# Macaron block on one core: the strands' normalizations, FFN sums, output scales and masks put on ScalarE and GpSimd beside the attention

## The chip, the cores and the metric

One core of one Trainium2 chip. The time is device microseconds (us) of one execution. Engines as the profile names them: PE is TensorE's matrix multiplication (PEld its weight loads), DVE VectorE, ACT ScalarE, POOL GpSimd, SP SyncE, which here only issues DMAs. PEclk is the TensorE clock that the throttle granted, as a share of full speed. L251 is line 251 of the kernel before.

## What is computed

x is (2, 1024, 512) in fp32. The block is a "macaron": half an FFN, attention, half an FFN, each on the normalized x and added to x.

```python
x = x + 0.5 * ffn(layernorm(x))
x = x + attn(layernorm(x))
x = x + 0.5 * ffn(layernorm(x))

def bitnet_linear(x, weight, scale):          # q, k, v and o projections
    s = maximum(mean(abs(weight), axis=1), 1e-8)
    y = einsum('bsi,oi->bso', x, sign(weight / s[:, None])) * (s * scale)
    return nan_to_num(y, nan=0.0, posinf=1e6, neginf=-1e6)

def attn(x):                                  # 32 query heads, 8 key/value heads, head size 16
    q, k, v = (bitnet_linear(x, w, sc) for w, sc in ...)
    p = softmax(q @ k.T / sqrt(16))           # 1024 keys a query
    return bitnet_linear(p @ v, o_weight, o_scale)

def ffn(x):                                   # base layer plus 8 LoRA experts of rank 16
    w = top-2 of softmax(x @ W_router.T), renormalized
    return x @ W_base.T + b_base + 2 * lora(x, w)
```

## The kernel before

**Tiles.** x stays on chip: 2 batches x 2 groups of 512 tokens, each group 4 tiles of 128 tokens x 512 columns (`xg[b, g]`, `xt[:, t, :]`). Most work on a tile is thus one instruction of 128 partitions x 512 elements. The q, k, v and o projections and the scores use numbers split into a rounded part and a remainder (fp32r), so they take two matmuls where one would do.

**The attention** (L831 on) goes through 32 units: a batch, a half of its queries (512) and one of 8 key/value groups with its 4 query heads. A unit is 4 steps, 128 steps in all. A step issues, for three different units at once:
- m: the scores of 8 tiles (queries on partitions, 512 keys), two matmuls each (`m_tile`, L742), whose row maxima DVE takes, negated (L751). They run 5 steps ahead. After a unit's fourth step the maxima are gathered, transposed and sent through a DMA into `mq`.
- e: the scores of 8 tiles the other way round (128 keys on partitions, 512 queries), two matmuls (L781) and a third that subtracts the maxima (L785), then the exp on ACT (L787), as 8 tiles `es`.
- av: the 32 matmuls of the step before's exps with the values (L820) into one PSUM bank for the unit. After the unit's last, `unit_end` copies the bank to `avs` on ACT (L795) and stores it to DRAM.

PSUM has 8 banks: one for av, seven in a ring for all else.

**What sets the order.** The order of instructions on each engine is written out by the program; no scheduler changes it. A step follows a string of turns: FULL when a strand has matmuls ready, BARE when none has, LEAD_IN at the start. Between the attention's turns m, e and A stand slots in which something else may be issued: F for PE, V and W for DVE, C and D for ACT, and one for POOL and one for DMAs after every turn.

What goes in these slots are **strands**: Python generators, one for each tile's chain of work (FFN, normalization, projections, output). A strand yields the engine that its next instruction needs ("P", "v", "a", "g" for POOL, "d" for a DMA on SP), what that comes after, and since when. A planner (`Flow`) counts ticks, 64 for a step, and offers a strand its slot when a table of delays (`LATER`: for instance 16 from an ACT instruction to the DVE one that uses it, 30 from POOL to DVE, 0 from POOL to POOL) says that the data should be there; on POOL two strand instructions stand at least 10 ticks apart (`APART`). It also keeps a stock of buffers: `t=10` for tiles of 128 x 512, `m=3` for masks, six PSUM banks less four during the attention. `flow.free` is false during the attention and true before and after it. Where the planner is wrong about a time, the engine waits: these ticks only order the instructions.

Strands join the attention by step: from its start, `first(1, 0)` and `first(1, 1)`, the first FFN and the q, k, v tiles of batch 1; later `second(0, 0)`, `second(0, 1)` and `second(1, 0)`, the output projection and the second FFN of three of the four groups. Everything of `first(0, 0)` and `first(0, 1)` is spawned before it, and their last tiles reach into it; `final` and `last` of group (1, 1) end after it. Before a unit is placed (loads of its q and k, L687 and L692) `need` (L839) checks that its q and k tiles are finished, and before its first e turn that its v tiles are (`place_v`, L726 and L727, on POOL). If they are not, `need` offers all five engines to the strands again and again, with no attention turn between, until they have been issued.

**The strands that the change touches:**
- `finite` (L226 to L260), nan_to_num of one tile, run for each q, k and v tile and each output tile. With `fast` 0, the case of most tiles: POOL takes the part below zero, clamped (L249, min then max); DVE makes a mask that is 1 where y x 0 is 0, so where y is finite or large but no NaN or infinity (L251); POOL takes the part above zero (L253, max then min) and adds the two (L255); DVE copies y under the mask (`copy_predicated`, L259).
- `ln_T` (L270 on): from the row statistics, DVE adds eps (L278), POOL takes the power -0.5 (L281, `rstd`), then for each of 4 tiles DVE computes xn = (x - mean) x rstd (L288), PE transposes it (L293), ACT copies it (L297), and ahead of q, k and v DVE makes its remainder (L300).
- `base` in `ffn_tiles` (L410 to L434): POOL makes xb = x + bh, bh being half the bias (L414); four matmuls with the base weight (L419) and one with the LoRA part (L423); DVE takes x = 0.5 x pb + xb from the bank (L425); then a store on SP or the row statistics for the next normalization on DVE.
- `qkv_part` (L490 on): matmuls (L504 for q and k tiles, L521 for v), the scale on ACT (L509) or on DVE for v (L526), `finite`, and for q and k the rounded part on ACT (L534), the remainder on POOL (L537) and two stores to DRAM on SP (L543), from where the units load them.
- `o_proj` (L619 to L649): matmuls (L634), DVE scales by the output scale `osc` (L639), `finite`, POOL adds to x (L645), DVE takes row statistics. Its inputs are normalized before it in `normalize` (L561 on), with POOL products at L586 and L590.

Of the kernel before, what the change touches and what calls it, by code (L numbers as in the profile page):

```python
# [32 lines left out]
def macaron_kernel(ctx: ExitStack, tc: tile.TileContext, x_in, wbT, b_base, wrT, aT, bT,  # L33
# [16 lines left out]
    def t512(name, dt=F32):  # L50
        return tmp.tile([P, 512], dt, tag="t512", name=name)
# [174 lines left out]
    def finite(y, o, n, fast, back):  # L226
# [20 lines left out]
        else:  # L247
            yield "g", src, t
            nc.gpsimd.tensor_scalar(lo_, y, 0.0, -BIG, ALU.min, ALU.max)  # L249
            yield "v", src, t  # L250
            nc.vector.tensor_scalar(m_, y, 0.0, 0.0, ALU.mult, ALU.is_equal)  # L251
            yield "g", ""
# [17 lines left out]
    def ln_T(xt, n, mv, given, tiles, xs, rank):  # L270
# [9 lines left out]
        rstd = sm.tile([P, TG], F32, tag="rstd", name=f"rstd{n}{tiles[0]}", bufs=4)  # L280
        nc.gpsimd.tensor_tensor(rstd[:, own], ve[:, own], mhalf[:, own], ALU.pow)  # L281
        at = flow.t

        def part(t):
            yield "r", dict(t=1)
            yield "v", "g", at
            xn = t512(f"xn{n}_{t}")
            nc.vector.tensor_scalar(xn, xt[:, t, :], mv[:, t, 0:1], rstd[:, t:t + 1], ALU.subtract,  # L288
                                    ALU.mult)
            yield "P", "v", None, 1  # L290
            pt = bank(f"pt{n}_{t}").rearrange("p (c q) -> p c q", c=KC)
            for c in range(KC):
                nc.tensor.transpose(pt[:, c, :], xn[:, c * P:(c + 1) * P], ident)  # L293
            flow.give(t=1)
            yield "a", "P"
            tok = slice(t * P, (t + 1) * P)
            nc.scalar.copy(xT[:, :, tok], pt)  # L297
            if xL is not None:
                yield "v", "a"
                nc.vector.tensor_tensor(xL[:, :, tok], pt, xT[:, :, tok].bitcast(F32), ALU.subtract)  # L300
            flow.give(fb=1)
# [18 lines left out]
    def ffn_tiles(xt, name, rank, tiles, xT, hT, mv, given, mv2, summed, store, loads):  # L320
# [89 lines left out]
        def base(t):  # L410
            yield "r", dict(t=1)
            yield "g", ""
            xb = t512(f"xb{n}_{t}")
            nc.gpsimd.tensor_tensor(xb, xt[:, t, :], bh, ALU.add)  # L414
            for c in range(KC):
# [7 lines left out]
            nc.tensor.matmul(pb, hT[0][:, t * P:(t + 1) * P], lb, start=False, stop=True)  # L423
            yield "v", "P"
            nc.vector.scalar_tensor_tensor(xt[:, t, :], pb, 0.5, xb, ALU.mult, ALU.add)  # L425
            flow.give(t=1, fb=1)
            if store is not None:
                yield ("a" if flow.free else "d"), "v"
                (nc.scalar if flow.free else nc.sync).dma_start(store[t * P:(t + 1) * P, :],
                                                                xt[:, t, :])  # L430
            if mv2 is not None:
                yield "v", "v"
                stats(xt, t, mv2, n)
                summed.add(t)  # L434
# [184 lines left out]
    def o_proj(b, g, hs, rank, mv, given, fast=False):  # L619
# [5 lines left out]
        def part(t):  # L625
            yield "r", dict(t=3)
            wo = signs["o"]
            for c in range(KC):
# [7 lines left out]
                flow.lock = ss[t] if c < 2 else None  # L636
            yield "v", "P"
            y = t512(f"yo{n}_{t}")
            nc.vector.tensor_tensor(y, po, osc, ALU.mult)  # L639
            flow.give(fb=1)  # L640
            done.append(t)
            r = t512(f"ro{n}_{t}")
            yield from finite(y[:, :], r[:, :], f"o{n}_{t}", fast, ("v", flow.t))
            yield "v" if fast else "g", "v"
# [186 lines left out]
    def attention(chains, n0):  # L831
# [6 lines left out]

        def need(*keys):  # L839
            for _ in range(4000):  # L840
                flow.settle()
                if set(keys) <= ended:
                    return
# [6 lines left out]
        for n in range(n0, TU * len(units) + LEAD + 1):  # L850
# [12 lines left out]
            for pos, (kind, p, i) in enumerate(order):  # L863
# [7 lines left out]
                elif kind == "A":  # L871
                    if a:
                        a_part(a[0], a[1] * 2 + p // 2, p % 2)
                elif kind == "S":
# [148 lines left out]
```

## Time and profile before

| | us |
|---|---|
| median of 3 runs | 1261.95 (1256.4 to 1266.83) |
| the profiled execution, its own time | 1256.92 |
| its span on the core | 1255.2 |
| 0 to 156 us: load, binarized weights, first FFN and q, k, v of batch 0 | 156; PE 114.33, DVE 111.84, ACT 35.45, POOL 71.54 busy |
| 156 to 1184 us: attention with strands beside it | 1028 |
| 1184 to 1255.2 us: last group's output projection and FFN | 71.2; PE 54.08, DVE 38.67, ACT 6.04, POOL 8.00 busy |
| largest group on DVE: the row maxima, L751 | 1024 x 0.682 = 657.0 busy |
| largest group on ACT: the exps, L787 | 1024 x 0.599 = 546.9 busy |
| mean granted TensorE clock | 0.915 |

The page's first part gives each engine's busy time and its share of the span. A busy engine need not be the one that sets the time: an instruction counts as busy also where nobody waits for it. PE's busy time includes matmuls at a lowered clock, so the same work is longer where PEclk is low. In groups such as `L253 POOL TENSOR_SCALAR z<-y 128x512 ... x17`, the first name is the tile written and the second the tile read, then come the shape, the count, the busy time, the mean of one in ns, and the idle time before them with what ended it. The chain of waits follows the work that ended last back from its end: at each step to whatever released it, or to the instruction before it on its engine. The profile's fences below come in these forms.

### The profile page before, as it was taken

The numbers are of one execution on the slowest core, as the hardware profiler recorded it, in microseconds if no ns is written. First come the engines' busy times: TensorE is split into PE (matmuls) and PEld (weight loads), VectorE is DVE, ScalarE is ACT, GpSimd is POOL, SyncE is SP. The second block draws the span as 40 slices with busy tenths as digits, with TensorE's granted clock in tenths as the row PEclk, the third lists the DMA queues.
The fourth block names the chain that finished last, engine by engine and source line by source line (L and its number), as shares of the span: only waits on it lengthen the run. The fifth ranks groups of instructions, "written<-read, shape, count | busy, mean of one in ns | idle before, by whom it ended". The sixth has DMA issues, their size and how long they took to land.

```text
span 1255.2 us, 25499 instructions
## 1 busy us (share of the span) xinstructions
PE 1148.8 (92%) x10501; PEld 606.1 (48%) x10501; DVE 902.8 (72%) x1733; ACT 641.6 (51%) x1249; POOL 295.0 (24%) x302
## 2 busy tenths in 40 slices
PE   3988699999999999999999999999999999998868
PEld 3546355454454544444554445444455444545434
DVE  5578876767786777776677976777769677895273
ACT  2222255655554665565565666455557655566401
POOL 3135832000000340031555220241000300422110
PEclk8989588899986999987999899899989899999788
DMA  7010332121212222223132241122222422211110
GB/s 254 1 59 34 81 122 85 52 52 52 52 52 52 69 80 57 70 76 89 49 90 75 72 122 53 33 52 69 61 60 67 123 68 65 68 55 38 45 39 34
DMA packets 38708, 85.57 MB, mean 68 GB/s; under 512 B 7728, under 2 KB 10800, under 8 KB 34624
## 3 DMA queue, kind: packets, MB, share of 16 engines
q1 hardware_dynamic: 37184, 81.26, 22.4%
q8 instruction: 82, 1.34, 0.4%
q10 hardware_dynamic: 1152, 2.10, 0.4%
q0 software_dynamic: 256, 0.59, 0.3%
q14 instruction: 34, 0.28, 0.1%
HBM read 59.57 MB, written 23.84 MB: 66 GB/s over the span
## 4 chain that ended last, share of the span: by engine, by line
PE 70%; DVE 19%; issue 3%; DMA 2%; POOL 2%; ACT 1%; SPq 1%; POOLq 0%; ACTq 0%; DVEq 0%
PE av L820 20%; PE m L742 16%; DVE mn L751 11%; PE e L781 10%; PE pbf L419 5%; PE pbs L419 5%; PE e L785 4%; PE po L634 2%; PE phs L342 1%; DMA qd<-y 1%; PE pq L504 1%; PE pbf L423 1%; PE pv L521 1%; PE pbs L423 1%; DMA x<-in_x 1%
## 5 line engine op out<-in xcount | busy, mean ns | idle before, releaser
L751 DVE TENSOR_REDUCE mn<-m 128x1 f32<-128x512 f32 x1024 | 657.0, 682 | 230.0 <-PE m L742 221.4
L787 ACT ACTIVATE es<-e 128x512 f32<-128x512 f32 x1024 | 546.9, 599 | 425.6 <-PE e L785 401.4
L742 PE MATMUL m<-k,q 32*128 32x512 f32 x2048 | 492.1, 464 | 21.1 <-DVE mn L751 15.1
L781 PE MATMUL e<-q,k 32*128 32x512 f32 x2048 | 407.9, 474 | 8.3 <-DVE mn L751 6.9
L742 PEld LDWEIGHTS m<-k,q 32*128 32x128 f32 x2048 | 240.8, 196 | 153.0 <-issue 67.4
L820 PE MATMUL av<-es,vaug 128*32 128x256 f32 x4096 | 290.3, 416 | 16.4 <-issue 10.3
L781 PEld LDWEIGHTS e<-q,k 32*128 32x128 f32 x2048 | 185.1, 194 | 114.7 <-DVE mn L751 69.6
L785 PE MATMUL e<-mq,ones_r 2*128 2x512 f32 x1024 | 233.0, 431 | 3.7 <-DMA mq<-mT 3.7
L820 PEld LDWEIGHTS av<-es,vaug 128*32 128x32 f32 x4096 | 121.5, 116 | 154.5 <-issue 103.8
L785 PEld LDWEIGHTS e<-mq,ones_r 2*128 2x128 f32 x1024 | 125.6, 196 | 25.1 <-issue 13.7
L419 PE MATMUL pbf<-wb,xTf 128*128 128x512 f32 x128 | 68.9, 653 | 1.3 <-DVE mn L751 1.3
L419 PE MATMUL pbs<-wb,xTs 128*128 128x512 f32 x128 | 64.8, 618 | 1.2 <-DVE mn L751 1.2
L586 POOL TENSOR_TENSOR an<-an,rb 128x512 f32<-128x512 f32 x15 | 19.2, 1281 | 142.7 <-DMA rd<-rs 72.1
L249 POOL TENSOR_SCALAR loa<-y 128x512 f32<-128x512 f32 x17 | 12.7, 750 | 157.1 <-ACT y L509 147.5
L726 POOL MEMSET vaug<- 128x128 f32 x32 | 6.6, 206 | 137.7 <-PE av L820 137.6
L419 PEld LDWEIGHTS pbf<-wb,xTf 128*128 128x128 f32 x128 | 23.2, 203 | 30.1 <-issue 26.1
L419 PEld LDWEIGHTS pbs<-wb,xTs 128*128 128x128 f32 x128 | 21.5, 189 | 27.1 <-issue 22.9
L253 POOL TENSOR_SCALAR z<-y 128x512 f32<-128x512 f32 x17 | 34.1, 2008 | 1.8 <-DMA qd<-y 0.6
L249 POOL TENSOR_SCALAR loo<-yo 128x512 f32<-128x512 f32 x12 | 7.4, 613 | 113.7 <-DVE yo L639 110.0
L537 POOL TENSOR_TENSOR z<-z,y 128x512 fp32r<-128x512 f32 x17 | 21.9, 1293 | 51.0 <-ACT y L534 51.0
L590 POOL TENSOR_TENSOR anxL<-an,anxT 128x512 fp32r<-128x512 f32 x15 | 19.2, 1280 | 53.5 <-ACT anxT L588 53.4
L634 PE MATMUL po<-sign_o,anxT 128*128 128x512 f32 x64 | 29.4, 459 | 1.2 <-DVE mn L751 1.2
(193 smaller groups left out, 1008.3 us busy)
## 6 DMA issues: line engine op xcount, KB each, us to landing
k<-kd SPq DMA_DIRECT2D x31, 1024.0 KB
q<-qd SPq DMA_DIRECT2D x32, 256.0 KB
ad<-avs SPq DMA_DIRECT2D x32, 256.0 KB
x<-in_x SPq DMA_DIRECT2D x16, 256.0 KB
qd<-y SPq DMA_DIRECT2D x16, 256.0 KB
qd<-z SPq DMA_DIRECT2D x16, 256.0 KB
an<-ad SPq DMA_DIRECT2D x15, 256.0 KB
rb<-rd SPq DMA_DIRECT2D x15, 256.0 KB
```

The source lines that it names most:

```text
L249: nc.gpsimd.tensor_scalar(lo_, y, 0.0, -BIG, ALU.min, ALU.max)
L253: nc.gpsimd.tensor_scalar(o, y, 0.0, BIG, ALU.max, ALU.min)
L419: nc.tensor.matmul(pb, xT[:, c, t * P:(t + 1) * P], wb[:, c, :], start=(c == 0), stop=False)
L423: nc.tensor.matmul(pb, hT[0][:, t * P:(t + 1) * P], lb, start=False, stop=True)
L537: (nc.vector if fast else nc.gpsimd).tensor_tensor(lo, o, y, ALU.subtract)
L634: nc.tensor.matmul(po, hs[j][:, c, t * P:(t + 1) * P], wo[:, c, :], start=(c + j == 0), stop=(c + j == KC))
L742: nc.tensor.matmul(s["m", i], s["q"][rows, qt * P:(qt + 1) * P], s["k"][rows, 1 - p, kh * 512:(kh + 1) * 512], start=(p == 0), stop=(p == 1))
L751: nc.vector.tensor_reduce(s["mn"][:, h, qt, kh:kh + 1], s.pop(("m", i)), AX.X, ALU.max, negate=True)
L781: nc.tensor.matmul(t, s["k"][rows, 1 - p, kt * P:(kt + 1) * P], s["q"][rows, :], start=(p == 0), stop=False)
L785: nc.tensor.matmul(t, ones_r[two, :], s["mq"][two, :], start=False, stop=True)
L787: nc.scalar.activation(e, s.pop(("e", i)), AF.Exp, scale=HD ** -0.5)
L820: nc.tensor.matmul(s["av"][32 * h:32 * h + 32, cols], s["v"][:, kt, :], s["es"][kt * REP + h][:, cols], start=(kt + half == 0), stop=(kt + ...
```

## The change

Beside the attention (`flow.free` false), and for the mask wherever `finite` runs with `fast` 0, work of the strands changes engine:
- the mask is computed by POOL, right after the part below zero, in place of DVE;
- a normalization computes, once for each `ln_T`, neg = -mean x rstd in two small POOL instructions, and each xn is one ACT instruction, Identity with scale rstd and bias neg, in place of DVE;
- an FFN tile adds bh to x in place on POOL; ACT then copies half the bank to a tile `hb`, and POOL adds that to x, in place of DVE's sum from the bank;
- an output tile is copied from its bank by ACT and multiplied by `osc` in place on POOL, in place of DVE's product.

`need` becomes a case of a new `until(cond)`, which also stands ahead of a unit's first av turn: until the copy of the unit before's av bank has been issued, it offers the engines to the strands.

```diff
--- before.py
+++ after.py
@@ -247,8 +247,8 @@
         else:
             yield "g", src, t
             nc.gpsimd.tensor_scalar(lo_, y, 0.0, -BIG, ALU.min, ALU.max)
-            yield "v", src, t
-            nc.vector.tensor_scalar(m_, y, 0.0, 0.0, ALU.mult, ALU.is_equal)
+            yield "g", ""
+            nc.gpsimd.tensor_scalar(m_, y, 0.0, 0.0, ALU.mult, ALU.is_equal)
             yield "g", ""
             nc.gpsimd.tensor_scalar(o, y, 0.0, BIG, ALU.max, ALU.min)
             yield "g", "g"
@@ -279,15 +279,26 @@
         yield "g", "v"
         rstd = sm.tile([P, TG], F32, tag="rstd", name=f"rstd{n}{tiles[0]}", bufs=4)
         nc.gpsimd.tensor_tensor(rstd[:, own], ve[:, own], mhalf[:, own], ALU.pow)
+        calm = not flow.free
+        if calm:
+            yield "g", ""
+            neg = sm.tile([P, TG], F32, tag="neg", name=f"neg{n}{tiles[0]}", bufs=4)
+            nc.gpsimd.tensor_tensor(neg[:, own], mv[:, own, 0], rstd[:, own], ALU.mult)
+            yield "g", ""
+            nc.gpsimd.tensor_scalar(neg[:, own], neg[:, own], -1.0, None, ALU.mult)
         at = flow.t
 
         def part(t):
             yield "r", dict(t=1)
-            yield "v", "g", at
+            yield "a" if calm else "v", "g", at
             xn = t512(f"xn{n}_{t}")
-            nc.vector.tensor_scalar(xn, xt[:, t, :], mv[:, t, 0:1], rstd[:, t:t + 1], ALU.subtract,
-                                    ALU.mult)
-            yield "P", "v", None, 1
+            if calm:
+                nc.scalar.activation(xn, xt[:, t, :], AF.Identity, bias=neg[:, t:t + 1],
+                                     scale=rstd[:, t:t + 1])
+            else:
+                nc.vector.tensor_scalar(xn, xt[:, t, :], mv[:, t, 0:1], rstd[:, t:t + 1],
+                                        ALU.subtract, ALU.mult)
+            yield "P", "a" if calm else "v", None, 1
             pt = bank(f"pt{n}_{t}").rearrange("p (c q) -> p c q", c=KC)
             for c in range(KC):
                 nc.tensor.transpose(pt[:, c, :], xn[:, c * P:(c + 1) * P], ident)
@@ -410,8 +421,7 @@
         def base(t):
             yield "r", dict(t=1)
             yield "g", ""
-            xb = t512(f"xb{n}_{t}")
-            nc.gpsimd.tensor_tensor(xb, xt[:, t, :], bh, ALU.add)
+            nc.gpsimd.tensor_tensor(xt[:, t, :], xt[:, t, :], bh, ALU.add)
             for c in range(KC):
                 yield ("P", "P") if c else ("P", "", flow.t, 1)
                 if c == 0:
@@ -421,15 +431,24 @@
                 flow.lock = bs[t] if c < KC - 1 else None
             yield "P", "a", ready
             nc.tensor.matmul(pb, hT[0][:, t * P:(t + 1) * P], lb, start=False, stop=True)
-            yield "v", "P"
-            nc.vector.scalar_tensor_tensor(xt[:, t, :], pb, 0.5, xb, ALU.mult, ALU.add)
-            flow.give(t=1, fb=1)
+            if flow.free:
+                yield "v", "P"
+                nc.vector.scalar_tensor_tensor(xt[:, t, :], pb, 0.5, xt[:, t, :], ALU.mult, ALU.add)
+                flow.give(t=1, fb=1)
+            else:
+                yield "a", "P"
+                hb = t512(f"hb{n}_{t}")
+                nc.scalar.activation(hb, pb, AF.Copy, scale=0.5)
+                flow.give(fb=1)
+                yield "g", "a"
+                nc.gpsimd.tensor_tensor(xt[:, t, :], xt[:, t, :], hb, ALU.add)
+                flow.give(t=1)
             if store is not None:
-                yield ("a" if flow.free else "d"), "v"
+                yield ("a" if flow.free else "d"), "v" if flow.free else "g"
                 (nc.scalar if flow.free else nc.sync).dma_start(store[t * P:(t + 1) * P, :],
                                                                 xt[:, t, :])
             if mv2 is not None:
-                yield "v", "v"
+                yield "v", "v" if flow.free else "g"
                 stats(xt, t, mv2, n)
                 summed.add(t)
 
@@ -634,13 +653,19 @@
                     nc.tensor.matmul(po, hs[j][:, c, t * P:(t + 1) * P], wo[:, c, :],
                                      start=(c + j == 0), stop=(c + j == KC))
                 flow.lock = ss[t] if c < 2 else None
-            yield "v", "P"
+            yield "v" if fast else "a", "P"
             y = t512(f"yo{n}_{t}")
-            nc.vector.tensor_tensor(y, po, osc, ALU.mult)
+            if fast:
+                nc.vector.tensor_tensor(y, po, osc, ALU.mult)
+            else:
+                nc.scalar.copy(y, po)
             flow.give(fb=1)
             done.append(t)
+            if not fast:
+                yield "g", "a"
+                nc.gpsimd.tensor_tensor(y, y, osc, ALU.mult)
             r = t512(f"ro{n}_{t}")
-            yield from finite(y[:, :], r[:, :], f"o{n}_{t}", fast, ("v", flow.t))
+            yield from finite(y[:, :], r[:, :], f"o{n}_{t}", fast, ("v" if fast else "g", flow.t))
             yield "v" if fast else "g", "v"
             (nc.vector if fast else nc.gpsimd).tensor_tensor(xt[:, t, :], xt[:, t, :], r, ALU.add)
             flow.give(t=2)
@@ -837,9 +862,12 @@
         live = []
 
         def need(*keys):
+            until(lambda: set(keys) <= ended)
+
+        def until(cond):
             for _ in range(4000):
                 flow.settle()
-                if set(keys) <= ended:
+                if cond():
                     return
                 flow.t += 1
                 for kind in "Pvagd":
@@ -870,6 +898,8 @@
                         e_tile(e[0], e[1] * 2 * REP + i, p)
                 elif kind == "A":
                     if a:
+                        if a[0] and a[1] == p == 0:
+                            until(lambda: "av" not in st[a[0] - 1])
                         a_part(a[0], a[1] * 2 + p // 2, p % 2)
                 elif kind == "S":
                     if 0 < hold <= len(units):
```

The built program of the kernel after has 89 instructions fewer on DVE (21 q, k and v masks, 12 o masks, 16 FFN sums, 28 normalizations, 12 output scales), 56 more on ACT and 77 more on POOL (33 masks, 12 products, 16 sums, 16 small ones for neg); PE has as many as before, SP too.

## The prediction

> **What bounds the kernel now.** I read first the page's busy times and the clock row, then a table of stretches, then single groups, and last the one place where batch 0 hands over to batch 1.
>
> ```profile
> PE 1148.8 (92%) x10501; PEld 606.1 (48%) x10501; DVE 902.8 (72%) x1733; ACT 641.6 (51%) x1249; POOL 295.0 (24%) x302
> ...
> PEclk8989588899986999987999899899989899999788
> ```
>
> PE is the full engine; DVE has a quarter of its time free, ScalarE half, GpSimd (POOL) three quarters. That average hides stages, so I cut the span: the attention runs from 156 to 1184 us, 128 steps of 8 exps each (1024 exps), 1028/128 = 8.03 us a step. Three single steps, by stretch (columns as named; PEclk is the granted clock):
>
> ```profile
> core 0: us, PE busy (x) PEld busy (x) DVE busy (x) ACT busy (x) POOL busy (x), PEclk, DMA share, GB/s
> 156.00:1184.00 1028.00, 980.43 (x9838) 505.66 (x9839) 752.29 (x1390) 600.10 (x1154) 215.44 (x222) 0.93 0.24 67
> 278.40:285.70 7.30, 7.30 (x80) 3.46 (x84) 5.00 (x9) 4.24 (x8) 0.00 (x0) 1.00 0.01 2
> 363.80:369.40 5.60, 5.60 (x75) 2.74 (x77) 5.60 (x11) 4.28 (x8) 0.00 (x0) 1.00 0.12 47
> 923.60:933.00 9.40, 9.40 (x75) 3.90 (x77) 4.87 (x8) 4.36 (x8) 0.00 (x0) 0.51 0.01 3
> ```
>
> The first step has strand matmuls between the attention's: PE 7.30 of 7.30, DVE 5.00. The second has none: PE and DVE both cover it. The third is the same work at half clock: 9.4 us. So in a filled step DVE work is free until about 7.3 us; in a bare step it shows; and PE that lets go loses its clock. Of 128 steps 99 are filled and 29 bare, in both programs by the built order. Followed through 156 to 1184 us, the chain of waits gives the operations that the change takes from DVE only 1.4 (o masks), 1.2 (output scales), 1.1 (normalizations) and 0.8 us (q/k/v masks). But POOL has 13.5 us on that chain, most of it in one place, where the q/k tiles of batch 1 come due before its first unit:
>
> ```profile
> 623.54 1.28 POOL L537 TENSOR_TENSOR z<-z,y 128x512 fp32r<-128x512 f32 x1 [0.26 <-ACT y L534]
> 624.91 0.97 POOL L249 TENSOR_SCALAR loa<-y 128x512 f32<-128x512 f32 x1
> 625.96 1.97 POOL L253 TENSOR_SCALAR z<-y 128x512 f32<-128x512 f32 x1
> 628.01 1.29 POOL L255 TENSOR_TENSOR z<-z,loa 128x512 f32<-128x512 f32 x1
> 629.38 1.13 POOL L249 TENSOR_SCALAR loa<-y 128x512 f32<-128x512 f32 x1
> 630.58 1.92 POOL L253 TENSOR_SCALAR z<-y 128x512 f32<-128x512 f32 x1
> 632.58 1.28 POOL L255 TENSOR_TENSOR z<-z,loa 128x512 f32<-128x512 f32 x1
> ```
>
> and, in the chain of waits (start, length, what), its release:
>
> ```profile
> 633.89 0.73 DVE z L259
> 634.63 0.58 DVE mn L751
> 635.20 0.04 issue
> 635.25 0.49 PE m L742
> ```
>
> POOL is solid, DVE's copy (L259) stands waiting for it, the row maxima behind that copy wait, and PE, whose banks they hold, stands 1.43 us.
>
> **What the change takes away.** DVE loses 89 instructions: 21 q/k/v masks x 0.60, 12 o masks x 0.68, 16 FFN sums x 0.685, 28 normalizations x 0.61 and 12 output scales x 0.676, that is 12.6 + 8.1 + 11.0 + 17.1 + 8.1 = 57 us (means of their rows).
>
> ```profile
> L251 DVE TENSOR_SCALAR ma<-y 128x512 uint8<-128x512 f32 x17 | 10.3, 605 | 0.7 <-ACT y L509 0.7
> ...
> L639 DVE TENSOR_TENSOR yo<-po,osc 128x512 f32<-128x512 f32 x16 | 10.8, 676 | 0.7 <-PE po L634 0.7
> ```
>
> On the path lie 4.5 us of these by the chain. Bounds: 0, and about 29 us, if every o mask, output scale and second normalization (8.1 + 8.1 + 12 x 0.74) fell in a bare step. I take 6: the sums sit in filled steps like the one above, where even a sum and its statistics (1.54 us) leave DVE at 6.5 of 7.3.
>
> **What it adds to ScalarE.** 28 normalizations, 16 half-copies, 12 output copies. The copy from a bank is 0.60 (L795); the scaled evacuation L509 0.69; with a second per-row operand an estimated 0.78. Together 28 x 0.78 + 28 x 0.60 = 39 us on an engine busy 600 of 1028. Each may hold an exp, and so a bank, for its length; between 0 and 8 us of the path, I take 2. Behind them queue the exps and the copy of the finished sums (L795); the next unit's first sum waits for that copy in either program.
>
> **What it adds to POOL.** 33 masks, 12 scale products and 16 sums (1.28 each, as L586), 16 tiny negations (at most 1.04 each, the 128x4 power of L281). The mask on POOL has no row. Two-operation scalar rows of its shape are 0.61 (L249: min, max) and 1.92 to 2.0 (L253: max, min). The Trainium skill ("GPSIMD Engine Reference", section 4.1) has it that one-input work runs there at about line rate and only two-input work costs twice DVE's. L249 fits it; L253, also one-input, is at three times L249. By the rule a mask is 0.6; by L253 1.95. I take 1.95: it makes a flag and is no min-max pair, so the general row is nearer; both ends stay for the range. In-place sums with bh only free a buffer.
>
> **The handover, step by step.** Let T be the end of the last K tile's matmuls (606.1 before). In the built order that tile stands one step later, the V tile and three q tiles follow with hardly any attention work between, and four dependent copies (K, V, q0, q1) stand back to back in DVE's queue, ahead of all further maxima. As in the trace, POOL starts at T+3.0 and the V tile reaches it at T+12 (before: 617.89). Until then POOL does K: 0.69 + 1.97 + 2.0 + 1.37, and two attention products, 2.6, ready at T+11.6. From T+12: V 6.0 with its mask, q0 6.4 with its mask, an attention product 1.3, the low half of q1 1.2, K's remainder 1.35, and q1's mask, clamp and sum 5.3: together 21.6, so T+33.6. DVE copy 0.73 and one maximum 0.58: PE goes on at T+35. PE itself ends V at T+9.2, three q tiles (24 x 0.23 = 5.5) at T+14.9, and with 7 banks in turn gets about half a step (3 us) on: it stands from T+18 to T+35, 17 us, where it stood 1.9 before. **+15** (at 0.6 a mask: +11). K's and q's loads queue on SP behind these tiles' stores; the first unit of batch 1 uses them four steps later, so they stay covered: k16 was issued at 628 and first needed at 654, and moves no more than the stall.
>
> The rule that weighs against such a hole is in "TensorE: Matmul & The Clock Gate", Part 1: an idle window of 3.4 us throttles the clock to half until a busy window has passed. By it the restart costs up to 3.4 us at half speed, 1.7 us lost; by the row 923.60:933.00, a whole step at 0.51, 3.8. I take **+2**.
>
> **The o tiles.** POOL had 5.1 us each (0.61 + 1.92 + 1.32 + 1.28); with scale, mask and gaps 8.8. In the second and third groups they come one a filled step (7.45 us), so each puts POOL 1.35 us further back. The hand planner leaves 94 of 64 ticks a step, 10.9 us, from the ScalarE copy to the masked copy; the first needs 8.1, the fourth 12.2. 1.3 us late, three groups, some of it covered: **+2** (0 to 8).
>
> **The start** (109 to 153 us) is POOL-bound until 127.6 and DVE-bound after. Three masks ahead of the first waited copy put it at 128.7; DVE then has less to do and the first row statistics are out about 1.8 us sooner, but the next masked copy, behind six masks, ends at 156.5 and holds DVE. I take 0 (-6 with cheap masks, +1). After 1184 us nothing that runs there changes but the in-place sum: 0.
>
> **Sum.** 1256.9 (profiled; span 1255.2) - 6 + 2 + 15 + 2 + 2 + 0 = 1271.9. The median of the runs, 1261.95, lies 5 above that execution: **1277**.
>
> **Rivals.**
> *Cheap masks* (0.6 us). Then -6 - 5 (start) + 2 + 11 + 2 + 0 - 4 (o stages, where DVE is lighter and POOL in time) = 0: about 1262. For it: L249. Against: L253.
> *DVE was the real bound in the o and bare stages.* For it: 11.9% of the attention's chain are maxima, and steps with output tiles take 8.7 to 11 us. Then -29, the handover only +8 since DVE comes to it with no backlog: about 1241, faster. It decides from about 20 us of DVE work on the path. Against: bare steps with 0.87 and with 1.27 us of such work both take 5.61.
> *POOL becomes the bound more widely*: the masked copies of four q/k/v tiles more and of all 12 o tiles wait for a mask each, 16 x 1.95 = 31: about 1308. Against: 222 POOL instructions take 215 of 1028 us.
> That the work is not moved is excluded: the built program has the counts above.
>
> **How the numbers follow.** Mine 0.52 (own range 1266 to 1292), cheap masks 0.20, DVE bound 0.15, POOL bound 0.13. A change of under 1% can hardly be told from none in this kernel. Over 1% slower is above 1274.6: 0.40 of mine and the last, 0.53. Faster by over 1% (under 1249.3): the third and a rest of the second, 0.18. Between: 0.29. Range with one in ten out on each side: 1247 to 1305.
>
> **What would show it.** POOL's mask rows at about 1.95 us (0.6: the first rival). A hole on PE of over 10 us near 620 to 650 us, ended by DVE's L259 after POOL's L255 of the second q tile, with a half clock behind it. DVE's wait for POOL at L259 well above 5.8 us. Filled steps still at 7.3 us though DVE has less. I am wrong if the hole is absent, or if the o stages shorten by over 10 us.

## The result, and the profile after

The kernel after takes 1274.33 us (median of 12 runs, 1261.56 to 1295.88), the kernel before 1261.02 (12 runs). The ratio is 1.0084, interval 1.0055 to 1.0112 (comparisons here leave disturbed runs out): 10.6 us slower, where +15 was forecast. The profiled execution took 1261.77 us (span 1260.0) and is at the fast end of its runs, with a granted clock of 0.920 where the nine runs compared average 0.912; so its stages are compared with before's, and totals come from the runs.

The page of the kernel after, its busy times and its clock row:

```profile
PE 1142.7 (91%) x10501; PEld 603.4 (48%) x10501; DVE 859.7 (68%) x1644; ACT 673.3 (53%) x1305; POOL 399.1 (32%) x379
...
PEclk8989589999998989997979989999979999999689
```

DVE has 43 us less, ACT 32 more, POOL 104 more: the work moved as counted. The 57 us that the prediction took from DVE are counts times means; busy time counts instructions that overlap once, so it falls by less. (For the same reason 1024 maxima of 0.682 us make the 657.0 us busy of the table before, and not 698.) The table of stretches (columns as in the prediction): the attention's window, a filled step, a bare step, and then steps 55 and 56 at the handover to batch 1, which before took 23.8 us:

```profile
156.00:1184.00 1028.00, 973.22 (x9802) 504.52 (x9806) 716.27 (x1313) 630.17 (x1206) 312.62 (x297) 0.93 0.24 68
331.30:338.60 7.30, 7.30 (x80) 3.46 (x79) 5.80 (x11) 4.23 (x8) 0.00 (x0) 1.00 0.00 0
700.40:706.00 5.60, 5.60 (x76) 2.86 (x72) 5.52 (x10) 4.92 (x9) 5.44 (x6) 1.00 0.50 135
605.60:647.10 41.50, 27.71 (x213) 17.80 (x209) 16.01 (x25) 13.64 (x26) 37.46 (x27) 0.75 0.19 48
```

Filled and bare steps last as long as before, 7.3 and 5.6 us. In the last row POOL is busy 37.46 of 41.50 us and PE 27.71. POOL's timeline there (start, length, what), by the built order from the K tile on:

```profile
607.33 0.62 POOL L249 TENSOR_SCALAR loa<-y 128x512 f32<-128x512 f32 x1 [6.81 <-ACT y L528]
608.01 1.93 POOL L251 TENSOR_SCALAR ma<-y 128x512 uint8<-128x512 f32 x1
610.02 1.93 POOL L253 TENSOR_SCALAR z<-y 128x512 f32<-128x512 f32 x1
...
615.88 0.95 POOL L249 TENSOR_SCALAR loa<-yv 128x512 f32<-128x512 f32 x1
...
632.28 1.93 POOL L251 TENSOR_SCALAR ma<-y 128x512 uint8<-128x512 f32 x1
634.27 1.93 POOL L253 TENSOR_SCALAR z<-y 128x512 f32<-128x512 f32 x1
636.28 1.26 POOL L255 TENSOR_TENSOR z<-z,loa 128x512 f32<-128x512 f32 x1
```

and in the chain of waits the release at its end:

```profile
637.57 0.73 DVE z L259
638.30 0.58 DVE mn L776
638.89 0.04 issue
638.93 0.79 PE m L767
```

The K tile's matmuls end at 604.43 (T). POOL began at T+2.9, the V tile reached it at T+11.5, the copy that releases PE came at T+33.1 and PE went on at T+34.5; the prediction had T+3.0, T+12, T+33.6 and T+35. PE stood 8.26 us from 623.5 and 5.50 from 633.4. Before, the eight steps around this place (steps 50 to 57, each counted from its first exp) took 79.6 us; after, 96.1: +16.5. The waits in 603 to 650 us name both holders:

```profile
DVE z L259 <- POOL z L255: 15.7, 3, 7.0
...
PE e L806 <- ACT es L812: 8.3, 1, 8.3
ACT y L553 <- DVE z L259: 7.6, 1, 7.6
...
PE m L767 <- DVE mn L776: 5.5, 1, 5.5
```

Only the second gap is the predicted one, DVE's maxima behind a copy. In the first, exps stand behind ACT's rounding of a q tile (L553), which waits for DVE's copy of that tile, which waits for POOL: the same chain through another queue.

A second hole was not predicted. ACT stood 5.28 us before the fourth normalization of the second FFN, at 744.5 us:

```profile
744.50 0.81 ACT L296 ACTIVATE xns<-x,negs,rstds 128x512 f32<-128x512 f32 x1 [5.28 <-POOL an L605]
```

Its inputs had been there for long. None of them comes from the POOL product (L605) that released it, so the wait must be for the tile that it writes: one of the ring of 128x512 tiles, which that product still read. The product itself waited 4 us for a DMA. Before, DVE met this wait for 1.0 us and PE did not stop; on ACT the exps stand behind it. PE stopped 3.35 us, until 745.86, and the half clock lasted 17.1 us, from 744.9 on. Steps 70 to 72, around it, take 31.3 us where before they took 20.2.

### The profile page after: what moved, and what is told of

Read it like the earlier page. It is cut to its first block, busy times and chain, and to the rows that moved or that the text cites. A ratio compares the mean times of both kernels' runs of the same rounds, so it can differ in the third digit from the quotient of the medians.

```text
span 1260.0 us, 25519 instructions
## 1 busy us (share of the span) xinstructions
PE 1142.7 (91%) x10501; PEld 603.4 (48%) x10501; DVE 859.7 (68%) x1644; ACT 673.3 (53%) x1305; POOL 399.1 (32%) x379
## 4 chain that ended last, share of the span: by engine, by line
PE 66%; DVE 12%; POOL 10%; DMA 5%; issue 4%; ACT 1%; SPq 1%; POOLq 0%; DVEq 0%; ACTq 0%
PE av L845 17%; PE m L767 15%; PE e L806 10%; DVE mn L776 6%; PE pbf L429 5%; PE pbs L429 4%; PE e L810 4%; DMA rd<-rs 3%; PE po L653 2%; PE pq L523 2%; POOL ma L251 1%; PE phs L353 1%; PE pbf L433 1%; PE pbs L433 1%; POOL z L253 1%
## 5 line engine op out<-in xcount | busy, mean ns | idle before, releaser
L845 PE MATMUL av<-es,vaug 128*32 128x256 f32 x4096 | 282.7, 408 | 8.5 <-DVE idfs L386 3.6
L810 PE MATMUL e<-mq,ones_r 2*128 2x512 f32 x1024 | 230.3, 430 | 2.0 <-DMA mq<-mT 2.0
L845 PEld LDWEIGHTS av<-es,vaug 128*32 128x32 f32 x4096 | 118.7, 114 | 143.2 <-issue 88.4
L444 POOL TENSOR_TENSOR x<-x,hbf 128x512 f32<-128x512 f32 x8 | 10.2, 1280 | 174.4 <-ACT hbf L441 174.4
L605 POOL TENSOR_TENSOR an<-an,rb 128x512 f32<-128x512 f32 x15 | 19.2, 1285 | 123.8 <-DMA rb<-rd 121.8
L444 POOL TENSOR_TENSOR x<-x,hbs 128x512 f32<-128x512 f32 x8 | 10.3, 1283 | 106.1 <-ACT hbs L441 106.1
L249 POOL TENSOR_SCALAR loa<-y 128x512 f32<-128x512 f32 x17 | 13.7, 804 | 87.5 <-ACT y L528 86.9
L424 POOL TENSOR_TENSOR x<-x,bh 128x512 f32<-128x512 f32 x32 | 40.8, 1305 | 0.0
L259 DVE COPY_PREDICATED z<-ma,y 128x512 f32<-128x512 uint8 x20 | 21.1, 1055 | 24.7 <-POOL z L255 24.6
L553 ACT CAST y<-z 128x512 fp32r<-128x512 f32 x20 | 12.5, 623 | 44.5 <-DVE z L259 41.3
```

Source lines behind the costliest of these rows:

```text
L424: nc.gpsimd.tensor_tensor(xt[:, t, :], xt[:, t, :], bh, ALU.add)
L810: nc.tensor.matmul(t, ones_r[two, :], s["mq"][two, :], start=False, stop=True)
L845: nc.tensor.matmul(s["av"][32 * h:32 * h + 32, cols], s["v"][:, kt, :], s["es"][kt * REP + h][:, cols], start=(kt + half == 0), stop=(kt + ...
```

## The experiments

Each kernel is the one named with the edit shown; ratios are to the kernel before on the same chip. Theory A: the masks on POOL make the loss at the handover (A1 by POOL's serial time, A2 by the order that is built there). B: normalizations on ACT hold exps. C: POOL's load everywhere. D: DVE is the bound, so whatever lightens it gains. For the parts that gain, later: E, the sums loosen the order at the handover; F, the scales relieve DVE in the output tiles.

**Masks back on DVE** (kernel after):

```diff
-            yield "g", ""
-            nc.gpsimd.tensor_scalar(m_, y, 0.0, 0.0, ALU.mult, ALU.is_equal)
+            yield "v", src, t
+            nc.vector.tensor_scalar(m_, y, 0.0, 0.0, ALU.mult, ALU.is_equal)
```

> The kernel after, but every mask on DVE again; normalizations, FFN sums and output scales stay moved. In the built order the tiles at the handover to batch 1 stand as before the change: the V tile and three q tiles in separate steps, maxima between the four masked copies. Theory A (the masks make the loss, most of it in the hole at the handover, where PE stands 8.3 and 5.5 us in the kernel after and some 17 us are at half clock behind it): no gap on PE over 3 us between 600 and 650 us, and the time falls below the kernel before, by the 44 us that DVE still loses, of which 3 to 8 us lie on the path: ratio 0.994 to 0.999. Theory B (ScalarE's new work holds exps and banks, above all the wait at 742 us): the time stays above before, ratio 1.003 to 1.008.

Measured: ratio 0.9804 (0.9754 to 0.9853), median 1237.22. PE's longest gap at 600 to 650 us is 1.74 us. A's direction holds: the masks make the whole loss, and more. But the gain, 25 us, is three times the 8 us at A's far end: in this company the masks cost 0.028, some 35 us, and the other moves gain 25. Steps 50 to 57 in the kernel after and then in this one:

```profile
560.20:656.30 96.10, 78.67 (x678) 44.15 (x677) 51.77 (x85) 46.48 (x87) 49.54 (x39) 0.80 0.28 83
```

```profile
558.60:630.00 71.40, 66.95 (x662) 37.57 (x660) 51.13 (x87) 43.23 (x82) 39.03 (x33) 0.93 0.30 88
```

They differ by 24.8 us. The two profiles differ by 23.8 in all (spans 1260.0 and 1236.2), so as far as the profiles show, the masks' cost lies at the handover.

**Masks back at the handover only** (kernel after; the six tiles of batch 1, group 1):

```diff
-            yield "g", ""
-            nc.gpsimd.tensor_scalar(m_, y, 0.0, 0.0, ALU.mult, ALU.is_equal)
+            if n[:4] != "a1_1":
+                yield "g", ""
+                nc.gpsimd.tensor_scalar(m_, y, 0.0, 0.0, ALU.mult, ALU.is_equal)
+            else:
+                yield "v", src, t
+                nc.vector.tensor_scalar(m_, y, 0.0, 0.0, ALU.mult, ALU.is_equal)
```

> The kernel after with the masks of the six tiles of batch 1, group 1 alone back on DVE; 27 masks stay on POOL. The built order at the handover stays the one of the kernel after: K one step later, V and three q tiles in one step, four masked copies nearly back to back ahead of the maxima. Theory A1 (POOL's serial time for these tiles is the hole): POOL has 4 x 1.95 = 7.8 us less before the copy that releases PE, so the two gaps of 13.8 us together shrink to about 6, and the time falls by 8 to 12 us against the kernel after, to a ratio of 0.999 to 1.002 to before. Theory A2 (the order, with copies back to back, makes the hole, whatever a mask costs): the gaps stay over 11 us and the ratio over 1.005. Theory C (POOL's load of masks everywhere costs): six of 33 masks are worth 2 us, ratio 1.006.

Measured: 1.0039 (1.0001 to 1.0077), median 1268.82; gaps 5.42 and 2.88 us, 8.3 in place of 13.8. Gaps and ratio both lie between the ranges of A1 and A2. So 5.5 us of the hole go with the masks' serial time (A1, 7.8 expected), and the rest stays with the built order (A2): K a step later, V and three q tiles in one step, copies back to back.

**Cheap masks** (kernel after, same order):

```diff
-            nc.gpsimd.tensor_scalar(m_, y, 0.0, 0.0, ALU.mult, ALU.is_equal)
+            nc.gpsimd.tensor_scalar(m_, y, 1.0, 1.0, ALU.min, ALU.max)
```

> The kernel after in exactly its order; only the mask's operation on POOL is another, min with 1 and then max with 1, so that the mask is always 1 and a NaN or an infinity is no longer replaced: that part of the computation is left out. It asks whether the general two-operation form is what makes a mask dear (the min-max pair took 0.61 us at L249). If such a mask takes 0.6 to 0.8 us: theory A expects 4 x 1.2 = 5 us less hole at the handover (8 to 9 us of gaps), 4 to 6 us less before 150 us and 0 to 4 in the output tiles, together ratio 0.996 to 1.001, as the rival with cheap masks was worked out (1262 where before is 1262). If POOL were not on the path, nothing changes: ratio 1.008. If it still takes 1.9 us, the price is that of the flag tile, not of the pair, and nothing changes.

Measured: 0.9995 (0.9971 to 1.0018), the first rival's time, no change. By form, the mask's row in the kernel after and then in this one:

```profile
L251 POOL TENSOR_SCALAR ma<-y 128x512 uint8<-128x512 f32 x17 | 32.9, 1935 | 1.0
```

```profile
L251 POOL TENSOR_SCALAR ma<-y 128x512 uint8<-128x512 f32 x17 | 10.4, 613 | 1.0
```

The pair of operations sets the price, 1.94 against 0.61 us, and not the flag tile, which both kernels write. The first exp comes 7 us sooner than in the kernel after (147.7 for 154.6 us), and the gaps at the handover are 5.8 and 4.2 us.

**Second normalizations on DVE** (kernel after):

```diff
-        calm = not flow.free
+        calm = not flow.free and n[0] != "s"
```

> The kernel after with the 12 normalizations of the second FFN back on DVE, all else as after; its order up to 700 us is that of the kernel after, so the hole at the handover stays. Theory B (in the profile after, ACT stood 5.3 us at 739 us before the fourth of these, which waits for a tile that a POOL product still reads, which itself waits for a DMA; exps stood behind it, PE stood 3.35 us and then ran 17 us at half clock): that gap goes, and the steps 70 to 72 fall from 31 to about 20 us; ratio 1.000 to 1.004. Theory A: the gap goes but the clock makes up for it elsewhere and DVE takes 12 x 0.74 = 9 us again, ratio 1.006 to 1.010.

Measured: 0.9976 (0.9951 to 1.0001), median 1257.47, 13.6 us below the kernel after by the ratios and at or below B's range. Steps 70 to 72 fall from 31.3 to 21.8 us. No gap over 1 us is left from 650 to 900 us and the half clock behind it is gone; the hole at the handover stays (8.27 and 5.49). D falls here: DVE got 9 us of work back and the kernel is faster.

**Masks and second normalizations back** (kernel after, the first edit and the last):

```diff
-            yield "g", ""
-            nc.gpsimd.tensor_scalar(m_, y, 0.0, 0.0, ALU.mult, ALU.is_equal)
+            yield "v", src, t
+            nc.vector.tensor_scalar(m_, y, 0.0, 0.0, ALU.mult, ALU.is_equal)
...
-        calm = not flow.free
+        calm = not flow.free and n[0] != "s"
```

> The kernel after with all masks and the 12 normalizations of the second FFN back on DVE; still moved are 16 normalizations of batch 1, the FFN sums and the output scales. Theory B (an ACT normalization that waits for a tile holds exps, PE stops and loses its clock): the gap and half clock that the kernel with the masks back still had at 707 to 736 us go, time lost to the clock 85 to 92 us where it was 94; ratio 0.972 to 0.980. Theory D (what made the kernel with the masks back fast is the lighter DVE): 9 us of DVE work come back, ratio 0.983 to 0.990.

Measured: 0.9792 (0.9748 to 0.9835). Against masks back alone (0.9804) the second normalizations make no difference that can be told, though the half clock at 726 us went (10.2 to at most 3.4 us) and steps 70 to 72 fell from 27.2 to 19.9 us; other steps gave it back. The price of 13.6 us was one of the two changes together. B's range holds, but its cause is not shown here.

**Sums and scales only** (kernel after, all masks and normalizations back):

```diff
-            yield "g", ""
-            nc.gpsimd.tensor_scalar(m_, y, 0.0, 0.0, ALU.mult, ALU.is_equal)
+            yield "v", src, t
+            nc.vector.tensor_scalar(m_, y, 0.0, 0.0, ALU.mult, ALU.is_equal)
...
-        calm = not flow.free
+        calm = False
```

> The kernel after with all masks and all normalizations back on DVE; only the 16 FFN sums and 12 output scales stay on ACT and POOL. In its built order the handover is looser than in both kernels: the q tiles come one a step, with maxima between all masked copies. Theory A and B (moved masks and moved normalizations each cost, sums and scales gain): no gap over 2 us at 570 to 640 us, ratio 0.970 to 0.982. Theory D: 17 us of DVE work come back against the kernel with the masks back, ratio 0.984 to 0.992.

Measured: 0.9836 (0.9794 to 0.9878), at the edge between the theories: with 17 us of DVE work more than with the masks back it is 4 us slower by the ratios, whose intervals overlap. No gap over 1 us is left from 210 to 720 us, so the handover has no hole. But at 726.0 us PE stops for 4.0 us, 13.7 us of half clock follow, and steps 70 to 72 take 31.3 us, as in the kernel after, with no normalization on ACT at all:

```profile
728.83 0.62 ACT L607 CAST anxT<-an 128x512 fp32r<-128x512 f32 x1 [4.94 <-POOL an L605]
```

This is the rounded copy of the product itself, which every kernel makes on ACT; here it stands ahead of exps, and the product waits 4.0 us for the DMA. So theory B is too narrow: the second hole does not need a moved normalization, only an ACT instruction ahead of the exps that waits for the late product.

**Masks only** (kernel before):

```diff
-            yield "v", src, t
-            nc.vector.tensor_scalar(m_, y, 0.0, 0.0, ALU.mult, ALU.is_equal)
+            yield "g", ""
+            nc.gpsimd.tensor_scalar(m_, y, 0.0, 0.0, ALU.mult, ALU.is_equal)
```

> The kernel before with the masks on POOL and nothing else. In its built order the V tile and three q tiles stand in separate steps and maxima stand between the four masked copies, as before. Theory A1 (POOL's serial time, 1.95 us a mask): the copy of the fourth tile still comes 7.8 us later, PE's gaps between 600 and 660 us sum to 5 to 9 us, where before had 1.9; time without the clock's loss 4 to 8 us up, ratio 1.003 to 1.008. Theory A2 (the hole comes from the compressed order that masks and normalizations moved together give): gaps under 4 us there, ratio 0.996 to 1.002. Theory D: DVE 21 us lighter, ratio under 0.995.

Measured: 1.0014 (0.9993 to 1.0035). The waits of PE at 600 to 660 us:

```profile
PE m L742 <- DVE mn L751: 5.5, 3, 2.9
```

5.5 us, the longest 2.9: the gaps lie in A1's range, the ratio in A2's. Alone, in the loose order, moved masks cost next to nothing in all. By stage, that is a cost and gains: steps 50 to 57 take 89.0 us (79.6 before), the first two groups of output tiles, steps 58 to 65 and 73 to 82, 59.9 and 83.2 (62.8 and 87.3 before). On top of sums and scales they cost 0.015 (the next kernel against the last), on top of the normalizations too, 0.028.

**No normalizations moved** (kernel after):

```diff
-        calm = not flow.free
+        calm = False
```

> The kernel after with all 28 normalizations back on DVE; masks, sums and scales stay moved. Its built order at the handover is the loose one. Theory B: as with the second normalizations back, the clock's loss is 90 to 97 us in place of 112; with the looser handover the gaps there are 4 to 9 us in place of 13.8; ratio 0.984 to 0.993. Theory A1 alone (POOL's masks make the loss and the order does not matter): gaps still over 10 us and ratio 0.997 to 1.003.

Measured: 0.9987 (0.9964 to 1.0009): the ratio lies in A1's range, above B's, and the gaps lie in B's. The order is loose, yet gaps of 2.30 and 4.25 us stay at the handover, and one of 3.88 at 568 us is new. The chain of waits there:

```profile
556.34 12.99 DMA rb<-rd
569.33 0.07 issue
569.39 1.27 POOL an L605
570.67 0.03 issue
570.69 0.55 DVE xna L299
571.24 0.60 DVE mn L776
```

It is the ring tile once more, now ahead of DVE's maxima: the wait does harm on either engine when the DMA is late enough, and ACT is not its only place.

**Sums only** (sums and scales only, with the output scale of before):

```diff
-            yield "v" if fast else "a", "P"
+            yield "v", "P"
...
-                nc.scalar.copy(y, po)
+            nc.vector.tensor_tensor(y, po, osc, ALU.mult)
...
-                nc.gpsimd.tensor_tensor(y, y, osc, ALU.mult)
...
```

> Of the change only the 16 FFN sums on ACT and POOL (and bh added to x in place; the wait for the av copy stays); masks, normalizations and output scales on DVE. Sums and scales together gave 0.984: 9 us without the clock's loss and 11 us of that loss. The built order at the handover is already the loose one that both had. Theory E (the gain is that the looser order at 530 to 640 us leaves no gap there, and that comes with the sums): ratio 0.983 to 0.989. Theory F (it is DVE work in the output tiles, so the scales): 0.994 to 1.000.

Measured: 0.9846 (0.9798 to 0.9893). Theory E. Steps 50 to 57 in the kernel before, then in this one:

```profile
566.50:646.10 79.60, 74.30 (x663) 40.56 (x667) 52.16 (x90) 43.72 (x82) 38.78 (x33) 0.85 0.29 83
```

```profile
568.90:631.40 62.50, 61.99 (x645) 33.95 (x647) 48.11 (x81) 40.42 (x77) 30.64 (x27) 0.93 0.29 83
```

62.5 for 79.6 us: PE idle 0.5 in place of 5.3, the clock 0.93 in place of 0.85, and some strand matmuls fall in other steps. With the sums moved, the planner has the K and V tiles ready a step earlier and sets the q tiles one a step.

**Scales only** (sums and scales only, with the FFN sum on DVE; bh stays added in place):

```diff
-            if flow.free:
+            if True:
                 yield "v", "P"
                 nc.vector.scalar_tensor_tensor(xt[:, t, :], pb, 0.5, xt[:, t, :], ALU.mult, ALU.add)
...
```

> Of the change only the 12 output scales on ACT and POOL; masks, normalizations and sums on DVE. Its order at the handover is that of the kernel before. Theory E: 0.995 to 1.000. Theory F: the steps with output tiles (58 to 66 and 73 to 83) shorten by 4 to 8 us and lose less clock, ratio 0.983 to 0.993.

Measured: 0.9887 (0.9838 to 0.9937). Theory F too: the first group of output tiles takes 59.0 us in place of 62.8, the second 83.6 in place of 87.3; the handover is as before (79.7). (The first group takes 58.8 us with the sums alone as well, so its part need not be the scales'; the second takes 89.2 there.) Sums and scales do not add: together 0.9836, a gain some 13 us smaller than the two alone would make. The hole at 726 us, which only the kernel with both has, makes its steps 70 to 72 11.3 us longer than here (31.3 for 20.0), about as much as is missing.

**Normalizations only** (masks back, and the edits of the last two for sums and scales):

```diff
-            yield "g", ""
-            nc.gpsimd.tensor_scalar(m_, y, 0.0, 0.0, ALU.mult, ALU.is_equal)
+            yield "v", src, t
+            nc.vector.tensor_scalar(m_, y, 0.0, 0.0, ALU.mult, ALU.is_equal)
...
-            if flow.free:
+            if True:
...
-                nc.scalar.copy(y, po)
+            nc.vector.tensor_tensor(y, po, osc, ALU.mult)
...
```

> Of the change only the 28 normalizations on ACT; masks, sums and scales on DVE. Theory B (moved normalizations cost only where they meet a late tile): near the kernel before, 0.994 to 1.002, time without the clock's loss within 3 us of before's. If normalizations on ACT were the gain that the sums and scales did not explain (17 us of DVE): 0.983 to 0.992.

Inconclusive: its 22 runs scatter from 1241.70 to 1270.61 us. Their median, 1264.89, lies above before, and the ratio, 0.9963 (0.9932 to 0.9994), lies below it but rests on eight of the runs.

bh added in place and the wait ahead of a unit's first av turn are in every kernel here but the one with the masks only. They were never tried alone; with scales only and with normalizations only, which have both, the handover takes 79.7 and 79.0 us, so its gain is not theirs.

**Best, with the output masks on POOL** (masks and second normalizations back, with this):

```diff
-            yield "v", src, t
-            nc.vector.tensor_scalar(m_, y, 0.0, 0.0, ALU.mult, ALU.is_equal)
+            if n[0] == "o":
+                yield "g", ""
+                nc.gpsimd.tensor_scalar(m_, y, 0.0, 0.0, ALU.mult, ALU.is_equal)
+            else:
+                yield "v", src, t
+                nc.vector.tensor_scalar(m_, y, 0.0, 0.0, ALU.mult, ALU.is_equal)
```

> The fastest kernel so far (masks and second normalizations back on DVE, ratio 0.979) with the 12 masks of the output tiles on POOL again, as after. The prediction's step for the output tiles: POOL 8.8 us for a tile that comes every 7.45, 1.3 us late in three groups, +2 (0 to 8): ratio 0.979 to 0.984. If the masks cost wherever they are, 12 of 33 of the 15 to 16 us that all of them cost without the clock, 5 to 6 us: ratio 0.984 to 0.988. If DVE's 8 us fewer are worth more than POOL's: under 0.978.

Measured: 0.9752 (0.9708 to 0.9797), median 1228.62: the fastest, 2.5% below the kernel before. Twelve masks at 1.94 us on POOL cost nothing and may gain (0.9792 without; the intervals overlap), against theory C. The masks that cost are those of the q, k and v tiles, as far as these kernels tell: no kernel had those alone with the rest.

## Why the prediction was right, and where it was not

**The mask's price** (1.95 by L253, against the 0.6 of L249 that the rule in the Trainium skill's "GPSIMD Engine Reference", section 4.1, one-input work at about line rate, would keep): right, 1.94. The rule would have given 1262; with masks that do cost 0.61 us the kernel did take 0.9995 of before. The row against the rule decided the sign. Of the prediction's two reasons one held, the pair of operations; that it makes a flag costs nothing (0.61 with the same flag tile).

**The handover, +15 and +2 for the clock**: right in place, course and size, 16.5 us over the eight steps. Its cause was mis-weighted. PE's gaps of over 1 us at the handover, from the end of the K tile's matmuls through step 57, summed (us), by order and masks:

| | these tiles' masks on DVE | on POOL |
|---|---|---|
| order as before, or close to it | 1.4 (before), 1.7 (masks back) | 5.2 (masks only), 6.6 (no normalizations moved) |
| compressed order | 8.3 (masks back at the handover) | 13.8 (after) |

These kernels differ in other ways too, but masks make 4 to 5.5 us in either order, and the compressed order 7 to 9 with either masks. The prediction read and used this order but did not price it by itself. Nor are the 16.5 us the whole price: the other moves alone shorten these eight steps to 71.4 us, 8.2 below before, and the masks add 24.8. The first gap came through ACT's rounding of a q tile, a queue that the prediction had left out.

**The clock's restart, +2**: low. From 625.4 us, 2 us into this hole, the trace shows 20.5 us at half clock, six times the window of 3.4 us that the Trainium skill's "TensorE: Matmul & The Clock Gate", Part 1, states, where the prediction had one step at most. PE was busy in 8.7 us of it, 7.0 of them after its last restart. A bare step takes 9.4 us at half clock and 5.6 at full, so 40% of such time is lost; that makes an estimated 3.5 us here. Such stretches carry much of the difference between kernels: half clock with PE busy (its half-clock stretches cut with its busy ones) sums to 178 us in the profile of before, 154 in that of after and 130 in that of the best kernel. Of the 30.8 us between the spans of before and best, an estimated 19 are this. But "PE that lets go loses its clock" is not the whole of it: half clock also comes where PE has hardly stood. In this row of before, PE is busy throughout at 0.50, and in the 13.7 us ahead of it PE stood 0.24 us in all:

```profile
980.61:987.44 6.83, 6.83 (x58) 2.89 (x50) 4.32 (x7) 3.96 (x8) 0.00 (x0) 0.50 0.47 124
```

The prediction's own row 923.60:933.00 is such a stretch as well, with PE busy 9.40 of 9.40 us at 0.51. What starts the half clock there is open.

**ScalarE, +2 (0 to 8)**: mis-sized. In the kernel after, putting the second normalizations back gives 13.6 us; with the masks back, only 1.5, within the noise. The prediction asked how long an instruction holds ACT (0.78; measured 0.82) and not what it waits for: a ring tile held by POOL and a DMA. Nor is it the normalizations' own price, as the kernel with sums and scales only has the same hole through another ACT instruction.

**DVE's relief, -6 (0 to -29)**: the step that failed. Sums, scales and normalizations together give -25 (0.9804), the sums alone -19 (0.9846). That is the far end itself: the three terms named for the 29 (8.1, 8.1 and 12 x 0.74) sum to 25. The prediction counted removed operations that lie on the chain of waits. It left out that with operations gone the planner issues strands in other steps, and that the clock changes with it: at the handover 17.1 us went with the sums, PE's idle time from 5.3 to 0.5 us and the clock from 0.85 to 0.93. "The sums sit in filled steps" is true and did not matter: they moved the K and V tiles.

**The output tiles, +2 (0 to 8)**: wrong in sign. The groups at 656 and 769 us took 56.0 and 78.9 us where before had 62.8 and 87.3, 15.2 less. The first group before, and then after:

```profile
646.10:708.90 62.80, 60.09 (x613) 31.15 (x613) 51.58 (x91) 36.43 (x69) 24.70 (x23) 0.92 0.26 75
```

```profile
656.30:712.30 56.00, 54.28 (x605) 28.21 (x602) 47.62 (x82) 37.70 (x71) 40.25 (x32) 1.00 0.27 76
```

The prediction had named over 10 us as the sign that it was wrong. DVE's relief was worth more than POOL's load: the groups are shorter with the masks moved alone as well as with the scales moved alone. How much of it is DVE as the bound, as the second rival had it, is not shown, since the clock rose too, from 0.92 to 1.00 and in the second group from 0.94 to 0.98.

**The start, 0**: right, the first exp at 154.6 for 155.9 us; with cheap masks -8, where -6 was put.

**The sum**: +15 forecast, +10.6 measured, inside its range and nearest to its own case. But that is in good part luck, two errors that cancel: relief of -25 where -4 stood for DVE and ACT together, and a cost of the masks, in this company, of +35 where the handover, its clock and the output tiles had +19. Of the 35, the profiles show 24.8 at the handover and, summed up, about nothing elsewhere. The other 10 or so stay open: the profiled execution of the kernel after was 9 us faster than the mean of the runs compared, and no profile shows where those lose it.

## What to carry to other kernels

When work is moved to an idle engine, price its slowest form on that engine from the nearest row, and ask of each moved instruction what it can wait for and who stands behind it: one late transfer that held an instruction ahead of the exps made three steps 11 us longer. Where a planner orders the work, compare the built orders at the tightest place: most of what the sums gained came because they loosened it. Try the parts alone and together: here two of four paid, and twelve of 33 instructions of a third.

## What was not expected of the hardware

- On POOL a two-operation scalar instruction on 128x512 takes 0.61 us at its median as min, then max (L249, and the cheap mask, to a flag tile too), and 1.93 as max, then min (L253) or as mult, is_equal (L251).
- Half clock came in multiples of 3.4 us in every profile (3.4, 6.8, 10.2, 13.7, 17.1, 20.5 us). Around the PE gap of 3.35 us at 742.5 it lasted 17.1 us, and PE was busy in 16.0 of them, from 745.9 to 761.9, at 0.50.
